# ScalarE's arithmetic and four kinds of VectorE instructions kept in the program's order in a selective-scan and attention kernel

## The chip, the cores and the metric

The kernel runs on one core of a Trainium2 chip. The metric is the device time of one execution in microseconds, as the median of several runs. A core has TensorE (PE, with its weight loads shown apart as PEld), VectorE (DVE), ScalarE (ACT), GpSimd (POOL) and SyncE (SP, which here only issues DMAs).

## The reference, cut to what matters

For 32 sequences of 256 tokens with 256 channels, the output is the input plus a two-layer feed of a conditioning block. The conditioning block is a gated state-space scan with 512 inner channels and 16 states; then come two layers of windowed attention (8 heads of 64, window 128) with a gated feed-forward of 682 hidden units. All in float32.

```python
# conditioning block, per sequence
xr, gate = split(x @ W_in.T);  xr = xr + t_emb
xc = silu(causal_conv4(xr) + b_conv)
xn = (xc - mean) / sqrt(var + 1e-5) * ln_g + ln_b
Bm, Cm, dt = split(xn @ W_xproj.T)
dt = tanh(dt @ W_dt.T + b_dt) * 0.01
Ad = 1 + dt * (-tanh(A_log));  Bd = Bm * minimum(norm(xn), 1)
for t in tokens:
    h = clip(h * Ad[t] + Bd[t] * xn[t], -10, 10);  y[t] = Cm[t] @ h
z = (y + D * xn) * silu(gate) @ W_out.T
# two layers, on z
q, k, v = split(shift(z) @ wqkv)
q, k = rotary(l2norm(q) * qs), rotary(l2norm(k) * ks)
z = z + windowed_softmax_attention(q, k, v) @ wo
a, g = split(layernorm(shift(z)) @ w1 + b1)
z = z + (a * gelu(g)) @ w2 + b2
out = x + z
```

## The kernel before, in words

**Two streams of work.** The 32 sequences are four groups of 8 (`GB`). The scan of a group runs over 256 tokens in 8 chunks of 32 (`group_scan`). Attention and feed-forward run over 64 positions, one for each group, layer and sequence (`seqs`). The first group is scanned alone; after that the scan of group g+1 is laid beside the positions of group g; the last group's positions have no scan beside them.

**How the order is written down.** In `group_scan` an agenda says at which scan step each piece is traced: `at(s0 - 36 + 2 * ch, conv_th, c, ch)` is the Tanh of chunk c, channel block ch, 36 steps before the chunk begins. For positions, `stage(n, i, what)` says in which of 8 slots of position n a piece is traced. The last loop of the program goes over the slots, traces what stands in each, and then lets the scan go on by about two steps, so that 16 positions go with 256 steps, or two with a chunk. So the text of the program gives one order over all engines.

**Who decides the order on an engine.** The order of the text is not the order of the queues. A scheduler reads the traced program, reckons by its own model when each operand will be there, and lets an instruction go ahead of earlier ones of its engine if it takes it to be ready. `tc.keep_in_program_order(ins)` puts an edge without a wait from the last instruction traced on the same engine to `ins`: `ins` may not be queued before that one. It says nothing of later instructions. In the kernel before it stands at some table set-up on GpSimd, and at `scale_row` (L645 to L652) for all groups but the first.

**The pieces that the change and the prediction name.**

- `conv_in` (L425 to L436) adds the condition to a projection in PSUM (DVE, xr) and starts the convolution (POOL, acc); `conv_taps` (L442) adds three taps on VectorE; `conv_th` (L450) is a Tanh on ScalarE, th; `conv_out` (L455) makes xc.
- `norm_turn` (L494) transposes xc into a PSUM bank tp_x; `norm_stats` (L504 to L509) takes mean and variance on VectorE and a power of -0.5 on GpSimd into stat; `norm_shift` (L514, DVE) multiplies mean and stat; `norm_apply` (L521, ACT) reads tp_x and writes xn; `norm_affine` (L528, L529, POOL) multiplies and adds; `norm_out` (L533, L535) stores xn in DRAM (xnd) by SP and squares it on ScalarE, sq_x. Each stands two to five steps after the one before it.
- `length` (L541, L542) ends in a power on GpSimd; `figures` (L550, DVE) makes rhs of it two steps later.
- `load_rows` (L625, SP) loads a token's row xrep from xnd, spread over states, six steps ahead; `scale_row` (L646, ACT) multiplies it by beta two steps ahead; `step` (L656, DVE) is the recurrence h; `read_out` (L668, PE) takes y from four h.
- `gate_th` (L368, L706, ACT) copies the gate out of PSUM (sg) and takes a Tanh (th_g); `copy_y` (L757, ACT) copies the block's output (yo); `raw_copy` (L472, ACT) copies raw.
- `Attention.project` (L903) is ps_qkv; v is copied on ScalarE (v_sb, L1084); `rotated` takes a square on ScalarE (sq, L916), the rotary products on VectorE (rot L919, swp L924), and three products and powers on GpSimd (L927, L935, L936); `turn` (L942, L947) transposes and copies into qT and kT on ScalarE.
- `scores` (L1102, L1109, L1118) ends in Exp on ScalarE (pT); `sums` (L1128, L1136) gives the inverse of the row sums; `values` (L1147, L1154) multiplies with v and copies into oT on ScalarE; `put_inverse` and `load_inverse` (L1159, L1166, SP) send the inverse through DRAM and back, spread over partitions, as rb, in slots 0 and 2 of the next position; `divide` (L1170, DVE) multiplies oT by rb in slot 4; `finish` (L953, L961) is ps_wo and the residual in slot 6.
- `FeedForward.normalise` (L1187 to L1197) ends in a power on GpSimd, rstd; `apply` (L1203, DVE) is hn; `spread` (L1215, L1217) transposes and writes hT on ScalarE; `widen` (L1238, L1246) is pa and a Gelu on ScalarE, ag; `product` (L1254, DVE) multiplies the two; `narrow` (L1266, L1277) is po_f and the residual on VectorE.

All PSUM tiles share one pool of eight banks (`ps_w`, tag "w"). xn, th and acc have two buffers each, xrep six, oT and rb one.

Of the kernel before, what the change touches and what calls it, by code (L numbers as in the profile page):

```python
# [13 lines left out]
AF = mybir.ActivationFunctionType  # L14
# [59 lines left out]
def kernel(  # L74
# [139 lines left out]
    for i in range(2):  # L214
        t = const.tile([P, NI * (P + GB)], FP, tag=f"ly{i}", name=f"ly{i}")
        nc.gpsimd.memset(t, 0.0)
        ly.append(t)

    def program(ctx, exact):
        rpool = ctx.enter_context(tc.tile_pool(name="res", bufs=1, reuse_waits="tile"))  # L220
        wpool = ctx.enter_context(tc.tile_pool(name="weights", bufs=1, reuse_waits="tile"))
# [12 lines left out]
        def constants(at):  # L234
# [75 lines left out]

            def decay_rate():

                nc.scalar.activation(a_sb, a_sb, AF.Tanh)
                nc.vector.tensor_scalar(a_sb, a_sb, -1.0, 0.01, ALU.mult, ALU.mult)

            def load_later():
# [48 lines left out]

        def reorder(out, ps):

            nc.scalar.copy(  # L368
                out.rearrange("p (q i b) -> p b i q", q=NQ, b=GB),
                ps.rearrange("p (b i q) -> p b i q", q=NQ, b=GB),  # L370
            )

        def group_scan(g):
# [73 lines left out]
            def conv_th(c, ch):  # L447
                acc = ck[c]["xr", ch][1]
                th = sp.tile([P, GB * CH], FP, tag="th", name="th", bufs=2)
                nc.scalar.activation(th, acc.rearrange("p b t -> p (b t)"), AF.Tanh, scale=0.5)  # L450
                ck[c]["th", ch] = th

            def conv_out(c, ch):
# [15 lines left out]

            def raw_copy(c):  # L470
                raw = sp.tile([4 * NS, GB * CH], FP, tag="raw", name="raw")
                nc.scalar.copy(raw, ck[c].pop("pr")[0 : 4 * NS, 0 : GB * CH])  # L472
                ck[c]["raw"] = raw

            def raw_turn(c):
# [35 lines left out]

            def norm_shift(c, j):
                stat, mv = ck[c]["stat"], ck[c].pop(("mv", j))
                nc.vector.scalar_tensor_tensor(  # L514
                    stat[:, j, 1:2], mv[:, 0:1], -1.0, stat[:, j, 0:1], ALU.mult, ALU.mult
                )

            def norm_apply(c, j):
                tp, stat = ck[c].pop(("tp", j)), ck[c]["stat"]
                xn = sp.tile([P, DI], FP, tag="xn", name="xn", bufs=2)  # L520
                nc.scalar.activation(  # L521
                    xn, tp, AF.Identity, bias=stat[:, j, 1:2], scale=stat[:, j, 0:1]
                )
                ck[c]["xn", j] = xn
# [6 lines left out]
            def norm_out(c, j):  # L531
                xn = ck[c].pop(("xn", j))
                nc.sync.dma_start(out=ck[c]["xnd"][j * P : (j + 1) * P], in_=xn)  # L533
                sq = sp.tile([P, DI], BF, tag="th", name="sq_x", bufs=2)
                nc.scalar.activation(  # L535
                    sq, xn, AF.Square, accum_out=ck[c]["ss"][:, j : j + 1]
                )

# [6 lines left out]
            def figures(c):  # L545
                stat = ck[c].pop("stat")
                ck[c]["rhs"] = []
                for j in range(NJ):
                    rhs = sm.tile([P, 3, CH], FP, tag="rhs", name="rhs")
                    nc.vector.tensor_mul(rhs, bc(tok_step, 1, 3), bc(stat[:, j], 2, CH))  # L550
                    ck[c]["rhs"].append(rhs)

            def figures_out(c):
# [26 lines left out]

            def decay_th(c):
                ad = sm.tile([P, CH], FP, tag="ad", name="ad")
                nc.scalar.activation(ad, ck[c]["bcd"][:, 2], AF.Tanh, bias=wbias[:, 2:3])
                ck[c]["ad"] = ad

            def decays(c):
# [113 lines left out]
            def gate_th(c, ch):  # L700
                if ch == 0:
                    ck[c]["sg"] = sp.tile([P, NC_, GB * CH], FP, tag="sg", name="sg")
                sg = ck[c]["sg"][:, ch]
                reorder(sg, ck[c].pop(("ps", NC_ + ch)))
                th = sp.tile([P, GB * CH], FP, tag="th", name="th_g", bufs=2)
                nc.scalar.activation(th, sg, AF.Tanh, scale=0.5)  # L706
                ck[c]["th_g", ch] = th

            def gate_out(c, ch):
# [44 lines left out]

            def copy_y(c, d):
                yo = sp.tile([P, GB, CH], FP, tag="yo", name="yo", bufs=2)
                nc.scalar.copy(  # L757
                    yo.rearrange("p b (i q) -> p q i b", q=NQ),
                    ck[c].pop(("po", d))[:, 0 : GB * CH].rearrange(
                        "p (q i b) -> p q i b", q=NQ, b=GB  # L760
                    ),
                )
                ck[c]["yo", d] = yo
# [148 lines left out]
        def rotated(l, ps, w, a):  # L912


            sq = ap_.tile([P, DI], FP, tag="swp", name="sq", bufs=3)
            nc.scalar.activation(sq, ps, AF.Square)  # L916
            rot = ap_.tile([P, HEADS, DH], FP, tag="rot", name="rot", bufs=4)
            ph = ps.rearrange("p (h d) -> p h d", h=HEADS)
            nc.vector.tensor_mul(rot, ph, bc(rc_sb[:, l, w, a], 1, HEADS))  # L919
            swp = ap_.tile([P, HEADS, DH], FP, tag="swp", name="swp", bufs=3)  # L920
            hd = DH // 2
            for i in range(2):
                o, s = slice(i * hd, (i + 1) * hd), slice((1 - i) * hd, (2 - i) * hd)
                nc.vector.tensor_mul(  # L924
                    swp[:, :, o], ph[:, :, s], bc(rs_sb[:, l, w, a, o], 1, HEADS)
                )
            nc.gpsimd.tensor_add(rot, rot, swp)  # L927
            ss = aw.tile([P, HEADS], FP, tag="ss", name="ss")
            nc.vector.tensor_reduce(
                ss, sq.rearrange("p (h d) -> p h d", h=HEADS), AX.X, ALU.add  # L930
            )

            nc.vector.tensor_scalar_max(ss, ss, 1e-24)  # L933
            rn = aw.tile([P, HEADS], FP, tag="rn", name="rn")
            nc.gpsimd.tensor_tensor(rn, ss, neg_half, ALU.pow)  # L935
            nc.gpsimd.tensor_mul(rot, rot, bc(rn, 2, DH))  # L936
            return rot

        def turn(rot, dst):
            tr = ps_w.tile([P, HEADS // 2, W], FP, tag="w", name="tr_qk")  # L940
            for hp_ in range(HEADS // 2):
                nc.tensor.transpose(  # L942
                    tr[:, hp_, :],
                    rot[:, 2 * hp_ : 2 * hp_ + 2, :].rearrange("p h d -> p (h d)"),
                    ident,
                )
            nc.scalar.copy(dst, tr)  # L947

        def project_out(b, oT):
            po = ps_w.tile([P, KM, S], FP, tag="w", name="ps_wo")  # L950
# [25 lines left out]
        def attention(l):  # L976

            for b in range(GB):

                qTs, kTs, vs = [], [], []  # L980
                for w in range(NW):
                    for a in (2, 0, 1):
                        ps = project_qkv(b, w, a)
                        if a == 2:
                            v_sb = ap_.tile([P, DI], FP, tag="v1", name="v_sb", bufs=3)
                            nc.scalar.copy(v_sb, ps)
                            vs.append(v_sb)
                            continue
                        rot = rotated(l, ps, w, a)
                        dst = ap_.tile(  # L990
                            [P, HEADS // 2, W], FP, tag="kT1" if a else "qT1",
                            name="kT" if a else "qT", bufs=3 if a else 2,
                        )
                        turn(rot, dst)
                        (kTs if a else qTs).append(dst)
                        yield

                oT = ap_.tile([P, NC_, S], FP, tag="oT", name="oT", bufs=1)
                for w in range(NW):
# [6 lines left out]
                    for h0 in range(0, HEADS // 2, nh):  # L1006
                        for r in range(2):
# [19 lines left out]
                                nmax[:, hsl], p_sb, AX.X, ALU.max, negate=True  # L1027
                            )
                            for i, h in enumerate(hs):
                                nc.scalar.activation(  # L1030
                                    p_sb[:, i, :], p_sb[:, i, :], AF.Exp,
                                    bias=nmax[:, h : h + 1],
                                    accum_out=rsum[:, h : h + 1],
# [34 lines left out]
        class Attention:  # L1068
# [7 lines left out]
            def project(self, b, w, a):  # L1076
# [4 lines left out]
                    ] + [ap_.tile([P, NW, DI], FP, tag="v", name="v_sb")]  # L1081
                ps = project_qkv(b, w, a)
                if a == 2:
                    nc.scalar.copy(self.qkv[b][2][:, w], ps)  # L1084
                else:
                    self.rot[b, w, a] = rotated(self.l, ps, w, a)

# [6 lines left out]
            def scores(self, b, kw, i0, n):  # L1094
# [20 lines left out]
                        )  # L1115
                for r in range(2):
                    p = aw.tile([P, n, nq], FP, tag="pT", name="pT", bufs=6)
                    nc.scalar.activation(p, banks[r], AF.Exp)  # L1118
                    for i in range(n):
                        self.p[b, kw, i0 + i, r] = p[:, i, :]  # L1120

# [17 lines left out]
            def values(self, b):  # L1139
                oT = ap_.tile([P, NC_, S], FP, tag="oT", name="oT", bufs=1)  # L1140
                for i0 in range(0, HEADS // 2, 2):
                    ov = ps_w.tile([P, 2, S], FP, tag="w", name="ov")
                    for i in range(2):
                        for kw in range(NW):
                            for r in range(2):
# [5 lines left out]
                                    start=(kw == 0),  # L1151
                                    stop=(kw == NW - 1),
                                )
                    nc.scalar.copy(oT[:, i0 : i0 + 2], ov)  # L1154
                self.o[b] = oT

            def put_inverse(self):
# [9 lines left out]
                self.rb = rb  # L1167

            def divide(self, b):
                nc.vector.tensor_mul(self.o[b], self.o[b], self.rb)  # L1170

            def finish(self, b):
                project_out(b, self.o.pop(b))
# [1 line left out]
        class FeedForward:  # L1175
# [24 lines left out]
            def apply(self, w):  # L1200
                tp, mv, rstd = self.hn[w]
                hn = ap_.tile([P, DM], FP, tag="hn", name="hn")
                nc.vector.tensor_scalar(  # L1203
                    hn, tp[:, 0:DM], mv[:, 0:1], rstd, ALU.subtract, ALU.mult
                )
                self.hn[w] = hn

            def spread(self, w):
# [5 lines left out]
                    ks = slice(k * P, (k + 1) * P)  # L1214
                    nc.tensor.transpose(tp[:, ks], hn[:, ks], ident)  # L1215
                for k in range(KM):
                    nc.scalar.activation(  # L1217
                        self.h[:, k, w * W : (w + 1) * W],
                        tp[:, k * P : (k + 1) * P],
                        AF.Identity,  # L1220
# [4 lines left out]
            def widen(self, m):  # L1225
# [17 lines left out]
                        stop=(k == KM - 1),  # L1243
                    )
                ag = aw.tile([P, S], FP, tag="ag", name="ag", bufs=7)
                nc.scalar.activation(ag[0:n], pg, AF.Gelu, bias=b1g)  # L1246
                self.pa[m] = pa, ag

            def product(self, m):
# [275 lines left out]
```

## Time and profile before

| | |
|---|---|
| median of 3 runs | 3857.5 us (3853.15 to 3862.57) |
| the profiled execution | 3861.79 us |
| span in its profile | 3860.0 us |
| PE busy | 3671.3 us, 95%, 20028 matmul records |
| PE weight loads | 2261.0 us, 59% |
| VectorE busy | 2629.5 us, 68%, 5177 instructions |
| ScalarE busy | 2163.9 us, 56%, 3769 instructions |
| GpSimd busy | 1754.4 us, 45%, 1776 instructions |
| DMA | 387.54 MB, 100 GB/s on average |
| the chain that ended last | PE 48%, DVE 20%, POOL 13%, DMA 8%, ACT 6%, issue 4% |

The profile is of one execution on the core. Its span runs from the first instruction to the last. A busy share is an average over stages with different limits. A line of a list of waits names the waiting engine and tile with its line of code, then an arrow to what came last, then the total in us, how often, and the longest. The chain of waits is followed back from the last instruction; in order of time its lines show a start, a length and what filled it. Ends of matmuls are modelled in such a profile, and matmuls overlap, so a busy PE is not a PE at its peak.

### The profile page before, as it was taken

How to read it: one execution, taken by the hardware profiler on the slowest of the kernel's cores; microseconds unless marked ns; L12 is line 12 of the kernel's file. 1: busy time of each engine (PE TensorE's matmuls, PEld its weight loads, DVE VectorE, ACT ScalarE, POOL GpSimd, SP SyncE). 2: the span in 40 equal slices, each digit the busy share in tenths (PEclk: the TensorE clock that was granted, in tenths of full speed). 3: DMA queues.
4: the chain of work that ended last, by engine and by line, in shares of the span. 5: the costliest groups of instructions: out<-in, count | busy, mean ns of one | idle time of the engine just before them, and what ended most of it. 6: DMA issues, size and time to landing. Idle time of an engine off the chain costs nothing.

```text
span 3860.0 us, 57026 instructions
## 1 busy us (share of the span) xinstructions
PE 3671.3 (95%) x20028; PEld 2261.0 (59%) x20028; DVE 2629.5 (68%) x5177; ACT 2163.9 (56%) x3769; POOL 1754.4 (45%) x1776
## 2 busy tenths in 40 slices
PE   7999889999999999999999999999999999999998
PEld 3333345665665665665666566566556666666666
DVE  6988887777777766777767677776777544444443
ACT  3555556565666656656655655565666444444442
POOL 4433465454454454454445445444444443443441
PEclk8999999999999999999999999999999999999999
DMA  5444554443444545334444544434344112011101
GB/s 152 115 118 117 145 140 120 111 117 98 117 125 118 139 115 140 106 99 113 107 120 110 128 121 128 120 95 111 105 117 126 51 45 62 12 28 37 30 25 35
DMA packets 396251, 387.54 MB, mean 100 GB/s; under 512 B 176355, under 2 KB 256052, under 8 KB 395828
## 3 DMA queue, kind: packets, MB, share of 16 engines
q1 hardware_dynamic: 311506, 371.80, 36.0%
q10 hardware_dynamic: 84450, 12.01, 2.0%
q8 instruction: 161, 2.64, 0.3%
q14 instruction: 134, 1.10, 0.1%
HBM read 348.05 MB, written 34.08 MB: 99 GB/s over the span
## 4 chain that ended last, share of the span: by engine, by line
PE 48%; DVE 20%; POOL 13%; DMA 8%; ACT 6%; issue 4%; SPq 1%; ACTq 0%; POOLq 0%; DVEq 0%
PE ps_qkv L903 9%; PE pa L1238 9%; PE po_f L1266 6%; DVE h L656 6%; POOL rn L935 5%; PE y L668 4%; DMA rb<-inv 3%; DVE acc L442 3%; PE ps_wo L953 3%; PE ov L1147 3%; PE sc L1109 3%; ACT xrep L646 2%; POOL rot L936 2%; DVE rot L919 2%; PE ps_in L395 2%
## 5 line engine op out<-in xcount | busy, mean ns | idle before, releaser
L656 DVE CUSTOM_DVE_ANT_0 h<-h,xrep,lim 128x512 f32<-128x512 f32 x1024 | 941.7, 920 | 133.8 <-ACT xrep L646 96.8
L903 PE MATMUL ps_qkv<-qkv,res 128*128 128x512 f32 x1536 | 715.0, 602 | 27.9 <-DVE ag L1254 18.2
L646 ACT ACTIVATE xrep<-xrep,beta 128x512 f32<-128x512 f32 x896 | 622.7, 718 | 139.3 <-DMA xrep<-xnd 99.1
L1238 PE MATMUL pa<-hT,w 128*128 128x256 f32 (+1 forms) x3072 | 684.5, 385 | 1.0 <-DVE zT L737 1.0
L1238 PEld LDWEIGHTS pa<-hT,w 128*128 128x128 f32 (+1 forms) x3072 | 497.8, 178 | 161.1 <-issue 42.3
L927 POOL TENSOR_TENSOR rot<-rot,swp 128x512 f32<-128x512 f32 x256 | 337.0, 1316 | 415.0 <-DVE swp L924 259.8
L935 POOL TENSOR_TENSOR rn<-ss,neg_half 128x8 f32<-128x8 f32 x256 | 453.4, 1771 | 28.0 <-DVE ss L933 17.5
L903 PEld LDWEIGHTS ps_qkv<-qkv,res 128*128 128x128 f32 x1536 | 278.9, 191 | 306.5 <-issue 263.0
L1266 PE MATMUL po_f<-ag,w 128*128 128x256 f32 (+1 forms) x1536 | 397.8, 401 | 40.0 <-DVE res L1277 16.6
L1197 POOL TENSOR_TENSOR rstd<-ve,neg_half 128x1 f32<-128x1 f32 x128 | 81.3, 635 | 771.3 <-DVE ve L1195 767.7
L668 PE MATMUL y<-h,ly 128*32 128x512 f32 x2048 | 381.1, 618 | 11.6 <-DVE h L656 10.9
L1254 DVE SCALAR_TENSOR_TENSOR ag<-pa,b_sb,ag 128x256 f32<-128x256 f32 (+1 forms) x448 | 213.0, 476 | 256.8 <-ACT ag L1246 254.3
L1266 PEld LDWEIGHTS po_f<-ag,w 128*128 128x128 f32 (+1 forms) x1536 | 279.7, 194 | 152.7 <-issue 43.6
L1246 ACT ACTIVATE ag<-pa,b_sb 128x256 f32<-128x256 f32 x320 | 150.7, 471 | 287.0 <-PE pa L1238 285.2
L936 POOL TENSOR_TENSOR rot<-rot,rn 128x512 f32<-128x512 f32 x256 | 294.5, 1150 | 20.0
L395 PE MATMUL ps_in<-xg,w_in_sb 128*128 128x256 f32 x1024 | 283.4, 406 | 15.1 <-DMA xg<-in_xT_dram 13.0
L916 ACT ACTIVATE sq<-ps_qkv 128x512 f32<-128x512 f32 x256 | 151.5, 596 | 238.9 <-PE ps_qkv L903 195.2
L395 PEld LDWEIGHTS ps_in<-xg,w_in_sb 128*128 128x128 f32 x1024 | 187.8, 197 | 146.8 <-issue 58.5
L442 DVE SCALAR_TENSOR_TENSOR acc<-xr,wc_sb,acc 128x256 f32<-128x256 f32 x384 | 187.8, 491 | 94.0 <-POOL acc L431 92.0
L953 PE MATMUL ps_wo<-oT,wo 128*128 128x256 f32 x1024 | 231.7, 379 | 0.0
L919 DVE TENSOR_TENSOR rot<-ps_qkv,rc_sb 128x512 f32<-128x512 f32 x256 | 175.0, 684 | 82.1 <-ACT sq L916 81.9
L1118 ACT ACTIVATE pT<-sc 128x512 f32<-128x512 f32 x384 | 208.5, 596 | 38.3 <-PE sc L1109 36.9
(146 smaller groups left out, 5479.9 us busy)
## 6 DMA issues: line engine op xcount, KB each, us to landing
xrep<-xnd SPq DMA_DIRECT2D x896, 256.0 KB
rb<-inv SPq DMA_DIRECT2D x128, 256.0 KB
xnd<-xn SPq DMA_DIRECT2D x64, 256.0 KB
qkv<-in_wqkv_dram SPq DMA_DIRECT2D x24, 512.0 KB
xd<-xnd SPq DMA_DIRECT2D x192, 64.0 KB
w<-in_w_dram SPq DMA_DIRECT2D x80, 128.0 KB
xg<-in_xT_dram SPq DMA_DIRECT2D x64, 128.0 KB
ys<-yo ACTq DMA_DIRECT2D x64, 128.0 KB
```

Of the source, the lines that this page charges most:

```text
L395: nc.tensor.matmul(ps, w_in_sb[:, k, ch * P : (ch + 1) * P], ck[c]["xg"][:, k], start=(k == 0), stop=(k == KM - 1),)
L442: nc.vector.scalar_tensor_tensor(acc, xr[:, :, k : k + CH], wc_sb[:, ch, k : k + 1], acc, ALU.mult, ALU.add,)
L646: scaled = nc.scalar.activation(bx, ck[c].pop(("bx", t), bx), AF.Copy, scale=ck[c]["beta"][:, t : t + 1])
L656: nc.vector._custom_dve(TENSOR_ADD_SAT, out=h_new, in0=state["h"], in1=bx, s0=ck[c]["lim"][:, 0, t : t + 1], s1=ck[c]["lim"][:, 1, t : t + 1],
L668: nc.tensor.matmul(ck[c]["y", hb][32 * q : 32 * q + 32, :], ly[hb % 2][:, 32 * t : 32 * t + 32], ck[c].pop(("h", hb * TB + t)), start=(i = ...
L903: nc.tensor.matmul(ps, res[b][:, k, t0 : t0 + W], wt["qkv", a][:, k], start=(k == 0), stop=(k == KM - 1),)
L927: nc.gpsimd.tensor_add(rot, rot, swp)
L935: nc.gpsimd.tensor_tensor(rn, ss, neg_half, ALU.pow)
L936: nc.gpsimd.tensor_mul(rot, rot, bc(rn, 2, DH))
L953: nc.tensor.matmul(po[:, d], wt["wo", 0][:, c, d * P : (d + 1) * P], oT[:, c, :], start=(c == 0), stop=(c == NC_ - 1),)
L1238: nc.tensor.matmul(pg if x else pa, wt["w1", m][:, k, x], self.h[:, k], start=(k == 0), stop=(k == KM - 1),)
L1266: nc.tensor.matmul(self.po[:, d], wt["w2", 0][r0 : r0 + n, m, d * P : (d + 1) * P], self.ag[m][r0 : r0 + n], start=(m == 0), stop=(m == le ...
```

## The change

Two small helpers, `activation` and `copy`, call ScalarE's instruction and pass it to `tc.keep_in_program_order`. All calls of `nc.scalar.activation` and `nc.scalar.copy` become calls of these, except in `scale_row`, which stays as it was: held for groups 1 to 3 and free for group 0. DMAs that ScalarE issues are not held themselves. Four kinds of VectorE instructions are held in the same way: `norm_shift` (L514), `figures` (L550), `divide` (L1170) and `apply` (L1203). Line numbers after the helpers grow by seven and more; on ScalarE the profile of the changed kernel shows the helpers' own lines.

```diff
+    def activation(*args, **kwargs):
+        return tc.keep_in_program_order(nc.scalar.activation(*args, **kwargs))
+
+    def copy(*args):
+        return tc.keep_in_program_order(nc.scalar.copy(*args))
...
             def conv_th(c, ch):
-                nc.scalar.activation(th, acc.rearrange("p b t -> p (b t)"), AF.Tanh, scale=0.5)
+                activation(th, acc.rearrange("p b t -> p (b t)"), AF.Tanh, scale=0.5)
...
             def norm_shift(c, j):
-                nc.vector.scalar_tensor_tensor(
-                    stat[:, j, 1:2], mv[:, 0:1], -1.0, stat[:, j, 0:1], ALU.mult, ALU.mult
+                tc.keep_in_program_order(
+                    nc.vector.scalar_tensor_tensor(
+                        stat[:, j, 1:2], mv[:, 0:1], -1.0, stat[:, j, 0:1], ALU.mult, ALU.mult
+                    )
                 )
...
             def norm_apply(c, j):
-                nc.scalar.activation(
+                activation(
                     xn, tp, AF.Identity, bias=stat[:, j, 1:2], scale=stat[:, j, 0:1]
                 )
...
             def figures(c):
-                    nc.vector.tensor_mul(rhs, bc(tok_step, 1, 3), bc(stat[:, j], 2, CH))
+                    tc.keep_in_program_order(
+                        nc.vector.tensor_mul(rhs, bc(tok_step, 1, 3), bc(stat[:, j], 2, CH))
+                    )
...
         def turn(rot, dst):
-            nc.scalar.copy(dst, tr)
+            copy(dst, tr)
...
             def divide(self, b):
-                nc.vector.tensor_mul(self.o[b], self.o[b], self.rb)
+                tc.keep_in_program_order(
+                    nc.vector.tensor_mul(self.o[b], self.o[b], self.rb)
+                )
...
             def apply(self, w):
-                nc.vector.tensor_scalar(
-                    hn, tp[:, 0:DM], mv[:, 0:1], rstd, ALU.subtract, ALU.mult
+                tc.keep_in_program_order(
+                    nc.vector.tensor_scalar(
+                        hn, tp[:, 0:DM], mv[:, 0:1], rstd, ALU.subtract, ALU.mult
+                    )
                 )
...
             def widen(self, m):
-                nc.scalar.activation(ag[0:n], pg, AF.Gelu, bias=b1g)
+                activation(ag[0:n], pg, AF.Gelu, bias=b1g)
```

The other replaced calls are those of `decay_rate`, `reorder`, `raw_copy`, `norm_out`, `decay_th`, `gate_th`, `copy_y`, `rotated`, `Attention.project`, `scores`, `values` and `spread`, and three in `attention`, which runs only where a bound on the scales of q and k does not hold; with these inputs it does not run.

## The prediction

> **What bounds the kernel now.** I read the busy times by stretch first, then the chain of waits in two places, then each engine's waits from 480 to 3000 us.
>
> ```profile
> 480.00:3000.00 2520.00, 2398.55 (x13599) 1519.86 (x13600) 1848.95 (x3611) 1512.68 (x2644) 1224.60 (x1211) 0.99 0.45 117
> 3000.00:3720.00 720.00, 719.82 (x4122) 480.72 (x4121) 326.11 (x701) 344.01 (x559) 303.04 (x258) 1.00 0.14 36
> 0.00:480.00 480.00, 423.62 (x1552) 166.54 (x1552) 405.31 (x762) 258.13 (x482) 196.51 (x280) 0.94 0.49 129
> ...
> 1584.68 0.70 PE po_f L1266 x2
> ...
> 1695.15 0.70 PE po_f L1266 x2
> ...
> 3304.78 3.45 PE ps_wo L953 x16
> ...
> 3346.35 3.45 PE ps_wo L953 x16
> ```
>
> The columns after the length are busy PE, PE weight loads, DVE, ACT and POOL. The run has three stages. To 480 us the scan of group 0 runs alone and VectorE is fullest (405 of 480). From 480 to 3000 us the scan of the next group runs beside attention and feed-forward: PE is busy 2398.55 of 2520 us, so it stands for 121.5 us, while VectorE is at 73% and ScalarE at 60%. From 3000 us on only attention and feed-forward are left, PE never stands, and a position (one sequence in one layer) takes 3346.35 - 3304.78 = 41.6 us. In the middle stage the chain repeats after two positions, 1695.15 - 1584.68 = 110.5 us, of which two bare positions are 83.1. The scan's matmul records per pair, at lengths from the same chain (64 of y at eight in 1.00, 16 of ps_out at eight in 1.94, 8 of ps_raw in 1.89, 32 of ps_in at four in 1.03, 16 of tz and tp_x at four in 0.59), fill about 24 us of the remaining 27. So a middle stage with no PE stall at all is worth about 3 us per pair where the pattern is regular, and 121.5 us with its irregular places. That is the ceiling of any gain there.
>
> ```profile
> PE ov L1147 <- DVE ag L1254: 21.9, 14, 2.6
> PE ps_qkv L903 <- DVE ag L1254: 18.2, 13, 1.4
> PE po_f L1266 <- DVE res L1277: 16.6, 10, 2.3
> ...
> DVE ag L1254 <- ACT ag L1246: 102.5, 60, 4.0
> DVE stat L514 <- POOL stat L509: 91.6, 39, 5.3
> DVE h L656 <- ACT xrep L646: 89.1, 81, 3.4
> DVE oT L1170 <- DMA rb<-inv: 82.8, 21, 5.8
> ...
> DVE rhs L550 <- POOL stat L542: 38.5, 23, 3.2
> DVE hn L1203 <- POOL rstd L1197: 34.1, 58, 1.8
> ...
> ACT th L450 <- DVE acc L442: 202.4, 68, 6.2
> ACT ag L1246 <- PE pa L1238: 141.9, 63, 6.8
> ACT sq L916 <- PE ps_qkv L903: 108.7, 100, 2.1
> ACT xn L521 <- DVE stat L514: 99.2, 36, 5.7
> ```
>
> These are total, times and longest wait in us, 480 to 3000. PE waits almost only for VectorE: its list adds up to 124 us, 104 of them on DVE, and mostly on a PSUM bank that VectorE has not yet read out. VectorE itself stands 649 us there: on four instructions whose input comes from GpSimd or a DMA (stat, oT, rhs, hn: 247), and on ScalarE (ag, h, and rot behind sq, 56.0: 248). ScalarE stands on th and xn, two scan instructions nobody is in a hurry for: I paired tiles in the trace, and between xn and the square that reads it lie 21 us in the median, between the division oT and the ps_wo matmuls more than 13 us in nineteen of twenty cases. These are heads of queues that hold up others and gain nothing.
>
> **What the Trainium skill says.** Perfetto Trace Analysis, "Tensor Engine Instruction (MATMUL, LD_WEIGHTS)": VectorE, ScalarE and GpSimd are strict FIFO, so a waiting head stops all behind it. The trace agrees: VectorE's 82.8 us before oT are idle though other work is queued. The same page, "Identifying the Most-Contended Engine": matmul busy time is no good measure of nearness to the limit. Here 95% PE busy hides the difference between the stages, which weight loads show (60% of the time in the middle, 67% after). PSUM — Partial Sum Buffer, "Terms": eight banks, a matmul output in one of them. From first matmul to last reader the trace has about 4.4 banks held on average in the middle stage, so a bank held longer is not at once a stall. ScalarE: Activation LUTs, "What ACT_TABLE_LOAD costs": about 1283 ns a load; the trace has 1283 ns, 248 times, 318 us.
>
> **The change, part by part.** No instruction is added or removed on any engine, and the built order has 248 table loads in both kernels: 0 us. Only orders move.
>
> ScalarE. All arithmetic but the 256 scale rows of group 0 (768 later ones were held already) now runs in the order of the text. Against before, in mean places of the queue: xn 10 later, th 3.2 later, sg and th_g 2 later, raw 2.2 later; sq 2.3, oT 3.0, qT and kT 2.6, ag 2.0 and v_sb 2.0 earlier. One instruction takes 1512.68/2644 = 0.57 us. Ten places are 5.7 us, against a mean wait of 99.2/36 = 2.8: the 99 us before xn go. th gets 1.8 us of cover against 202.4/68 = 3.0 us: about 60% of 202 goes, 122, and of the 43.1 us (13 times) that it waits behind ve about 20. That is 240 us of ScalarE's 1007 idle, 24%. They don't vanish, since ScalarE has work for 1513 us only: it will stand instead before PE's results (ag, sq, oT, qT), where it is early rather than late. VectorE's 248 us of waiting on ScalarE fall by the same 24%, 59 us.
>
> VectorE. In places: oT 18 later (2 to 36), stat 6.4 later, rhs 3.7 later, hn 1.3 earlier. One instruction takes 1848.95/3611 = 0.51 us. oT: 9.2 us of cover against a longest wait of 5.8, all 83 us go. stat: 3.3 us against 2.3 in the mean, about 80 of 91.6. rhs: 1.9 against 1.7, about 32 of 38.5. hn: nothing goes. Sum 195 us. What hides the lateness of oT is the reserve before ps_wo; were that gone, PE would wait for the division itself. With ScalarE's 59 that is 254 of 649 us, 39%.
>
> What PE gets. A share in proportion would be 39% of 121.5, 47 us; all of it 121.5. I take 60%, 73 us: the heads removed (2.3 to 3.9 us each) are longer than PE's waits (1.3 to 1.7 us each), so one removed head tends to remove a whole wait.
>
> GpSimd and SP. On SP the xnd write moves 4.3 places later, rb 0.8 earlier, the xrep loads 0.3 later; xn's two products on GpSimd move 3 later, rot 0.4 earlier. SP also waits in order, so an xnd write that comes late holds xrep loads; the 21 us after xn cover it. 0, at worst +10. Two banks per chunk (tp_x) are held some 15 us longer: 2 x 15 / 110 = 0.3 bank of eight; 0, at worst +15.
>
> First stage: VectorE bound, with 1.6 and 1.4 us of stat and rhs waits, so nothing to gain; th, waiting 45 us there, is not on VectorE's path. 0, from -10 to +15. Last stage: PE never stands, 0, at worst +10 if a strict ScalarE reaches an eviction late.
>
> Sum: -73. The profiled execution took 3861.8 us (span 3860.0), 4.3 above the median of the runs, so 3789 for it and 3857.5 - 73 = 3785 as a median.
>
> **Rivals.** *PE becomes the only bound* in the middle stage: -121.5, and some 30 more from matmuls following each other without restart: 3705. For it: after the change ScalarE waits for PE, not the reverse. Against: ag, h, hn and acc (76.9 behind GpSimd) still stop VectorE.
>
> *The waits are hidden anyway*: PE's stalls come from VectorE being 73% full in bursts, and with one head gone it stops at the next (acc, ag). Half the proportional share or less, -20: 3838. Against: 83 of the removed us are in single waits of 4 us.
>
> *Slower*: strict ScalarE puts the scale rows (L646) behind evictions that wait for PE. Per position four q/k turns and two oT copies have moved ahead; at 1.4 us of waiting each over 45 positions that is 378 us during which xrep is not made, and h (3.5 us of reserve in the median, under 0.8 in a quarter of its rows) stops VectorE. 378 - 195 = +183 us of VectorE waiting at 121.5/649 = 0.19 us each: +34, with +15 from the first stage and +10 from the last, 3917. It decides once VectorE's waits on ScalarE (248 us now) exceed 248 + 195 = 443.
>
> **How the numbers follow.** Forecast 0.52; PE bound 0.12; hidden 0.19; slower 0.17. The forecast's own range is 3740 to 3825. Leaving out the far halves of the two outer cases gives 3705 to 3880. About 0.2% (8 us) can be told from no change: of the hidden case a quarter lies within it, and a little of the slower one. Faster 0.77, same 0.07, slower 0.16.
>
> **What would show it.** oT, stat and rhs waits on VectorE near zero, th and xn waits on ScalarE cut by two thirds with ag, sq, oT and qT waits on PE grown; PE busy above 2440 per 2520 us in the middle; a pair of positions at 107 to 109 us; the last stage still 41.6 us a position. It is wrong if h behind xrep grows past 200 us, if PE waits on tp_x or ps_in banks, or if the last position starts no earlier.

## The result, and the profile after

| | before | after |
|---|---|---|
| median on the same chip | 3859.15 us (3853.15 to 3862.57, 4 runs) | 3802.81 us (3799.04 to 3807.15, 4 runs) |
| ratio | | 0.9856, 95% interval 0.9839 to 0.9873 |
| span of the profiled execution | 3860.0 us | 3805.3 us |
| PE busy, whole span | 3671.3 us | 3678.6 us |
| VectorE, GpSimd busy, whole span | 2629.5, 1754.4 us | 2685.8, 1845.0 us |

The change makes the kernel 56 us faster. First, the busy times by stretch after, from 480 us on (start and end, length, then busy PE, PE weight loads, DVE, ACT, POOL, the granted clock, the DMA share and GB/s):

```profile
480.00:3000.00 2520.00, 2467.15 (x13914) 1564.91 (x13913) 1938.76 (x3669) 1547.10 (x2692) 1329.27 (x1234) 0.99 0.46 117
3000.00:3720.00 720.00, 720.00 (x4163) 483.65 (x4163) 318.56 (x686) 339.83 (x553) 304.61 (x252) 1.00 0.14 36
```

PE now stands for 2520 - 2467.15 = 52.9 us in the middle instead of 121.5. Over the whole span (span less busy time) it stands for 126.7 us instead of 188.7, but is busy 7.3 us longer with the same 20028 matmul records. The last stage is full on PE, as before. The page's line for the chain that ended last, after:

```profile
PE 74%; DVE 14%; POOL 4%; ACT 3%; issue 2%; DMA 2%; SPq 0%; ACTq 0%; POOLq 0%; DVEq 0%
```

PE was 48% of it, GpSimd 13% and DMA 8%. The inverse sums on their way through DRAM (rb) are no longer in the chain; the powers on GpSimd (rn) still are, but seldom. The waits after, 480 to 3000 us (total, times, longest in us):

```profile
ACT ag L221 <- PE pa L1253: 272.7, 143, 5.1
ACT sq L221 <- PE ps_qkv L914: 147.8, 133, 1.8
DVE h L667 <- ACT xrep L657: 145.6, 109, 3.6
ACT oT L224 <- PE ov L1158: 134.0, 87, 7.2
...
DVE st L1204 <- PE tp_h L1200: 98.9, 40, 3.7
...
DVE rot L930 <- ACT sq L221: 63.4, 49, 2.9
...
ACT th L221 <- DVE acc L449: 37.5, 15, 6.6
...
DVE hn L1217 <- POOL rstd L1210: 31.6, 48, 3.1
DVE ag L1269 <- ACT ag L221: 29.2, 43, 2.5
...
DVE stat L522 <- POOL stat L516: 4.8, 2, 4.4
DVE rhs L560 <- POOL stat L551: 1.6, 1, 1.6
```

VectorE's wait for rb is gone from the list, and so is ScalarE's for the statistics before xn. ScalarE and VectorE now wait mostly for PE (ag, sq, oT; and st, which stood at 9.3 us before). One wait has grown that isn't on PE: h behind its scaled row xrep, from 89.1 to 145.6 us.

The chain in order of time after (start, length, what) repeats every 1662.66 - 1552.49 = 110.2 us in the middle, and every 41.6 us at the end:

```profile
1552.49 0.70 PE po_f L1281 x2
...
1662.66 0.70 PE po_f L1281 x2
...
3041.60 3.45 PE ps_wo L964 x16
3083.17 3.45 PE ps_wo L964 x16
```

In the regular places the pair was 110.5 us before, so it has hardly moved. What went are the irregular places. From the trace I took the start, in us, of the first ps_wo matmul of positions 14 and 40 (counted from 0), the same in each run below:

| | position 14 | position 40 | mean pair between |
|---|---|---|---|
| before | 1378.6 | 2848.7 | 113.1 us |
| after | 1351.7 | 2795.1 | 111.0 us |
| e1, all of ScalarE held, VectorE free | 1376.8 | 2833.3 | 112.0 us |
| e2, VectorE's four kinds held, ScalarE free | 1357.4 | 2773.3 | 108.9 us |
| e3, divide alone held | 1352.6 | 2794.0 | 110.9 us |
| e4, th and xn alone held | 1364.5 | 2783.1 | 109.1 us |
| e8, th, xn and divide held | 1339.8 | 2731.7 | 107.1 us |
| e5, th, xn and VectorE's four held | 1338.2 | 2724.8 | 106.7 us |
| e11, e5 with th free | 1339.9 | 2755.1 | 108.9 us |
| e7, e5 and the gate held | 1356.8 | 2746.3 | 106.9 us |
| e10, e5 and yo held | 1346.3 | 2731.7 | 106.6 us |
| e12, e5, gate and yo held | 1353.4 | 2793.3 | 110.8 us |
| e6, the change with gate and yo free | 1341.8 | 2727.6 | 106.6 us |
| e9, the change with yo free | 1344.5 | 2734.5 | 106.9 us |

"Mean pair" is the difference of the two columns over 13. Of what the change gains, 27 us are there by position 14 and another 27 come between 14 and 40. The twelve runs are told next.

### The profile page after: what moved, and what is told of

The parts are those of the page before. It is cut to its first block, busy times and chain, and to the rows that moved or that the text cites. A ratio compares the mean times of both kernels' runs of the same rounds, so it can differ in the third digit from the quotient of the medians.

```text
span 3805.3 us, 57114 instructions
## 1 busy us (share of the span) xinstructions
PE 3678.6 (97%) x20028; PEld 2274.6 (60%) x20028; DVE 2685.8 (71%) x5177; ACT 2170.2 (57%) x3769; POOL 1845.0 (48%) x1776
## 4 chain that ended last, share of the span: by engine, by line
PE 74%; DVE 14%; POOL 4%; ACT 3%; issue 2%; DMA 2%; SPq 0%; ACTq 0%; POOLq 0%; DVEq 0%
PE pa L1253 15%; PE ps_qkv L914 13%; PE po_f L1281 8%; PE y L679 6%; PE ps_wo L964 5%; DVE h L667 4%; PE ov L1158 4%; PE sc L1120 4%; PE ps_in L402 4%; PE ps_out L757 3%; PE tr_qk L953 3%; PE rs L1139 2%; DVE acc L449 2%; PE sc L1113 2%; DVE swp L935 1%
## 5 line engine op out<-in xcount | busy, mean ns | idle before, releaser
L667 DVE CUSTOM_DVE_ANT_0 h<-h,xrep,lim 128x512 f32<-128x512 f32 x1024 | 987.4, 964 | 182.9 <-ACT xrep L657 149.7
L1281 PE MATMUL po_f<-ag,w 128*128 128x256 f32 (+1 forms) x1536 | 389.9, 394 | 17.4 <-DVE ag L1269 14.9
L947 POOL TENSOR_TENSOR rot<-rot,rn 128x512 f32<-128x512 f32 x256 | 313.4, 1224 | 19.9
L449 DVE SCALAR_TENSOR_TENSOR acc<-xr,wc_sb,acc 128x256 f32<-128x256 f32 x384 | 188.7, 494 | 103.9 <-POOL acc L438 102.6
L1120 PE MATMUL sc<-qT,kT 64*128 64x128 f32 (+1 forms) x2048 | 239.2, 346 | 0.0
```

The costliest lines, as they stand in the source:

```text
L667: nc.vector._custom_dve(TENSOR_ADD_SAT, out=h_new, in0=state["h"], in1=bx, s0=ck[c]["lim"][:, 0, t : t + 1], s1=ck[c]["lim"][:, 1, t : t + 1],
L1120: nc.tensor.matmul(banks[r][:, i, :], kT[rows, i0 + i, kw * W : (kw + 1) * W], qT[rows, i0 + i, kw * W :], start=False, stop=(i == n - 1),)
L1281: nc.tensor.matmul(self.po[:, d], wt["w2", 0][r0 : r0 + n, m, d * P : (d + 1) * P], self.ag[m][r0 : r0 + n], start=(m == 0), stop=(m == le ...
```

## The experiments

**The two halves, and their likeliest parts.** Theory V: VectorE's heads (stat, rhs, oT, hn) carry the gain. Theory S: ScalarE's queue, freed of th and xn, carries it. e1 and e2 do one half of the change each.

```diff
 e1, against the change: each of the four VectorE kinds
-                tc.keep_in_program_order(
-                    nc.vector.tensor_mul(self.o[b], self.o[b], self.rb)
-                )
+                nc.vector.tensor_mul(self.o[b], self.o[b], self.rb)
 e2, against the change: ScalarE as it was
-        return tc.keep_in_program_order(nc.scalar.activation(*args, **kwargs))
+        return nc.scalar.activation(*args, **kwargs)
...
-        return tc.keep_in_program_order(nc.scalar.copy(*args))
+        return nc.scalar.copy(*args)
```

> All of ScalarE held, VectorE's four kinds free again. Theory V (the gain is VectorE's own four heads, 195 of the 254 us of waits in the prediction's sum, and a quarter of it ScalarE's): 10 to 20 us faster than before (ratio 0.995 to 0.997), VectorE's waits on oT, stat and rhs between 480 and 3000 us still near 83, 92 and 38 us. Theory S (the gain is ScalarE's queue freed of th and xn, so that Gelus, squares and copies come in time): 40 to 56 us faster (0.985 to 0.990), with the waits on oT, stat and rhs unchanged all the same.

> VectorE's four kinds held, ScalarE as before. Theory V: 35 to 50 us faster (0.987 to 0.991), waits on oT and stat near zero, and ScalarE still waiting some 200 us before th. Theory S: 5 to 15 us faster (0.996 to 0.999), since ScalarE still stands before th and xn and hands Gelus and squares to VectorE late. If the two parts need each other, both this and the run with ScalarE alone stay under half of the 56 us.

e3 is e2 with only `divide` held, e4 holds only th and xn and nothing on VectorE:

```diff
 e4, against e2 (VectorE's four free as well)
-                activation(th, acc.rearrange("p b t -> p (b t)"), AF.Tanh, scale=0.5)
+                tc.keep_in_program_order(
+                    activation(th, acc.rearrange("p b t -> p (b t)"), AF.Tanh, scale=0.5)
+                )
...
-                activation(
-                    xn, tp, AF.Identity, bias=stat[:, j, 1:2], scale=stat[:, j, 0:1]
+                tc.keep_in_program_order(
+                    activation(
+                        xn, tp, AF.Identity, bias=stat[:, j, 1:2], scale=stat[:, j, 0:1]
+                    )
                 )
```

> Only divide (oT by rb) held on VectorE, nothing else held. Theory V: its 83 us of waiting are 83/254 of the sum, so about 18 us faster (0.995), with the wait on rb near zero. Theory S: within 5 us of before, although the wait on rb goes: VectorE then stands at the next head (stat, ag, h) instead.

> Only the two ScalarE instructions th (conv_th) and xn (norm_apply) held, nothing on VectorE. Theory V: about 10 us faster (0.997). Theory S: 30 to 50 us faster (0.987 to 0.992), nearly all that holding the whole of ScalarE gives, because these two are the heads that stood in front of the others; waits of ScalarE before th and xn under a third of 202 and 99 us between 480 and 3000 us.

| | median | before, same chip | ratio, 95% interval |
|---|---|---|---|
| e1 | 3850.37 us | 3861.14 us | 0.9974 [0.9963, 0.9985] |
| e2 | 3774.20 us | 3861.14 us | 0.9776 [0.9763, 0.9789] |
| e3 | 3805.44 us | 3861.14 us | 0.9861 [0.9846, 0.9877] |
| e4 | 3798.76 us | 3861.14 us | 0.9846 [0.9828, 0.9864] |

VectorE's half alone gains 87 us, more than the whole change; ScalarE's half alone gains 11. So V had the order of these two right, and the size of e1; for e2 it had said 35 to 50. Neither theory had the other two: one VectorE kind alone (divide) gains 56 us, and two ScalarE kinds alone (th, xn) gain 62, where all ScalarE kinds gain 11. Nor did either foresee that in e1 VectorE's waits on oT, stat and rhs fall to 37.4, 68.0 and 19.1 us with nothing held there. Something among the other ScalarE kinds costs about 50 us. What VectorE's half leaves standing is seen in the waits of e2, 480 to 3000 us:

```profile
ACT th L221 <- DVE acc L449: 210.3, 72, 6.7
...
DVE h L667 <- ACT xrep L657: 203.2, 152, 3.4
...
ACT xn L221 <- DVE stat L522: 97.0, 26, 5.1
```

th and xn still stand at ScalarE's head as long as before (202.4 and 99.2), and h waits longer for its rows (203.2 us against 89.1). With th and xn alone held, e4, the same list has:

```profile
DVE stat L523 <- POOL stat L518: 88.5, 40, 5.3
...
DVE h L667 <- ACT xrep L657: 30.5, 34, 3.4
```

h waits a third as long as before, stat as long. The two repairs work on different waits.

**Only the parts that gained, and which part costs.** e5 holds th and xn (and one Tanh at set-up, `decay_rate`) on ScalarE and the four kinds on VectorE; all other ScalarE kinds are free. e6 is the whole change with sg, th_g and yo free, and so keeps attention's and the feed-forward's evictions held: theory E was that those evictions cost the 50 us. e7 is e5 with sg and th_g held. e8 is e5 with only `divide` held on VectorE.

```diff
 e6, against the change (e5 does the same to all kinds but th, xn and decay_rate)
-            copy(
+            nc.scalar.copy(
                 out.rearrange("p (q i b) -> p b i q", q=NQ, b=GB),
...
-                activation(th, sg, AF.Tanh, scale=0.5)
+                nc.scalar.activation(th, sg, AF.Tanh, scale=0.5)
...
-                copy(
+                nc.scalar.copy(
                     yo.rearrange("p b (i q) -> p q i b", q=NQ),
```

> The changed kernel with only th, xn (and the one-off decay rate) held on ScalarE; all other ScalarE instructions free, VectorE's four kinds held. Theory G (the part of the change that costs is holding the scan's other ScalarE work, above all sg, th_g and yo, which then stand in a burst right before a scale row): 90 to 105 us faster than before (0.973 to 0.977), a pair of positions at 107.5 us in the middle stage, VectorE's wait on xrep under 110 us between 480 and 3000 us. Theory C (th and xn held late are themselves the cost beside the four VectorE kinds, since xn late makes the chunk late): 45 to 65 us faster, as the whole change.

> The changed kernel with sg, th_g and yo free again on ScalarE; everything of attention and feed-forward still held. Theory G: 80 to 105 us faster than before (0.973 to 0.979). A rival, theory E (evictions of attention, moved ahead of scale rows, are the cost): no better than the change, 50 to 60 us faster, with VectorE's wait on xrep still above 140 us.

> th, xn and the gate's sg and th_g held on ScalarE, nothing else there; VectorE's four kinds held. Theory G with the gate as the piece: 50 to 70 us faster than before, so 30 to 45 us lost against the kernel with th and xn alone. Theory G with yo as the piece, or theory E: within 10 us of the kernel with th and xn alone.

> th and xn held on ScalarE, and of VectorE's kinds divide alone. If each head pays once, divide (56 us alone) and th with xn (62 us alone) would add up to 118 us; since PE stood for 121.5 us and the two share its waits I expect 75 to 95 us (0.975 to 0.981), and 5 to 20 us less than with all four kinds.

| | median | before, same chip | ratio, 95% interval |
|---|---|---|---|
| e5 | 3733.14 us | 3856.75 us | 0.9679 [0.9664, 0.9693] |
| e6 | 3738.78 us | 3856.75 us | 0.9693 [0.9679, 0.9707] |
| e7 | 3752.71 us | 3856.75 us | 0.9721 [0.9706, 0.9736] |
| e8 | 3739.44 us | 3856.75 us | 0.9692 [0.9678, 0.9705] |

e5 is the fastest version found: it beats the kernel before by 124 us and the change by some 68 (ratios 0.9679 and 0.9856). Theory G had said 90 to 105. e6 is within 6 us of it, inside the intervals, with every eviction of attention held, so theory E falls: with gate and yo free, the q/k turns, oT, sq and ag cost next to nothing in the text's order. The cost lies with the gate and yo. But the gate alone, e7, costs only 16 us by the ratios (0.0042; 20 by the medians), nearly all of it before position 14: the table has it 18.6 us behind e5 there and 21.5 at position 40. That is neither the 30 to 45 us of G with the gate as the piece nor the under 10 of its rivals.

e8 against e4 and e3: 62 and 56 us alone, 117 together, so th with xn and divide add up, where 75 to 95 had been expected. Stat, rhs and hn, worth 33 us on top of divide alone (e2 against e3: 0.0085), are worth 5 when th and xn are held (e5 against e8: 0.0013, inside the intervals).

**Where the cost sits in time.** I read one and the same place of the pair in the chain of the change and of e5, from the ps_qkv of four matmuls to the po_f matmuls. After (pieces left out between):

```profile
1595.08 1.93 PE ps_qkv L914 x4
...
1597.52 0.62 ACT yo L224
1598.13 0.49 ACT sg L224
...
1599.68 0.67 ACT xn L221
1600.35 0.62 ACT xrep L657
1600.99 1.73 DVE h L667
...
1608.49 0.49 DVE ag L1269
...
1612.18 0.70 PE po_f L1281 x2
```

and e5:

```profile
1570.93 1.72 PE ps_qkv L914 x4
...
1578.31 1.00 PE y L679 x8
1579.31 1.93 PE ps_in L402 x8
...
1582.98 2.98 PE po_f L1281 x12
```

From the end of ps_qkv to po_f the change needs 1612.18 - 1597.01 = 15.2 us, nearly all of them on ScalarE and VectorE; e5 needs 1582.98 - 1572.65 = 10.3, all on PE. ScalarE's own order there, after (start, length, engine and line, what, and in brackets the idle time before it with its releaser):

```profile
1589.09 0.72 ACT L657 ACTIVATE xrep<-xrep,beta 128x512 f32<-128x512 f32 x1
1593.05 0.47 ACT L221 ACTIVATE ag<-pa,b_sb 128x256 f32<-128x256 f32 x1 [3.24 <-PE pa L1253]
...
1597.04 0.58 ACT L224 COPY v_sb<-ps_qkv 128x512 f32<-128x512 f32 x1 [2.25 <-PE ps_qkv L914]
1597.52 0.62 ACT L224 COPY yo<-ps_out 128x256 f32<-128x256 f32 x1
...
1600.25 1.32 ACT L657 ACTIVATE xrep<-xrep,beta 128x512 f32<-128x512 f32 x2
```

and in e5:

```profile
1567.29 0.61 ACT L768 COPY yo<-ps_out 128x256 f32<-128x256 f32 x1 [2.32 <-PE ps_out L757]
...
1568.81 0.71 ACT L657 ACTIVATE xrep<-xrep,beta 128x512 f32<-128x512 f32 x1
...
1572.30 0.76 ACT L657 ACTIVATE xrep<-xrep,beta 128x512 f32<-128x512 f32 x1
1572.92 0.61 ACT L1095 COPY v_sb<-ps_qkv 128x512 f32<-128x512 f32 x1
```

The bank of yo is written by 1590.42 in the change (ps_out at 1588.50 for 1.92 us), but yo runs at 1597.52, because in the text it stands after the copy of v, and v waits for PE. The gate comes after yo, xn after the gate, and the next row xrep after all of them: 1589.09 to 1600.25 without a row. h stops, the products of VectorE behind it come late, and PE waits for the last of them. In e5 yo runs as soon as its bank is written, and rows go through between everything else. This recurs: between positions 14 and 40 yo starts 6.8 us after its bank is written in the median of 26 cases in the change, and 0.4 in e5.

**One link or the whole chain.** e9 frees yo alone in the change; e10 holds yo alone beside e5; e12 holds yo and the gate beside e5, with attention still free. e11 asks which of th and xn gains: it is e5 with th free.

```diff
 e9, against the change
-                copy(
+                nc.scalar.copy(
                     yo.rearrange("p b (i q) -> p q i b", q=NQ),
 e10, against e5
-                nc.scalar.copy(
+                copy(
                     yo.rearrange("p b (i q) -> p q i b", q=NQ),
 e12, against e10
-            nc.scalar.copy(
+            copy(
                 out.rearrange("p (q i b) -> p b i q", q=NQ, b=GB),
...
-                nc.scalar.activation(th, sg, AF.Tanh, scale=0.5)
+                activation(th, sg, AF.Tanh, scale=0.5)
 e11, against e5
-                activation(th, acc.rearrange("p b t -> p (b t)"), AF.Tanh, scale=0.5)
+                nc.scalar.activation(th, acc.rearrange("p b t -> p (b t)"), AF.Tanh, scale=0.5)
```

> The change with one kind of ScalarE instruction free again: copy_y (yo), everything else held. Theory Y (yo alone carries what e6 gave back: a held yo stands behind copies of later positions and keeps the scale rows waiting): ratio 0.970 to 0.975, about 3745 to 3760 us, pair of positions at 106.5 to 107, h waiting for xrep below 120. Rival G (gate and yo are only costly together, or gate alone puts the rows back): ratio 0.980 to 0.986, pair still near 110.

> e5 with copy_y (yo) held on ScalarE in addition. Theory Y: about 40 us lost against e5, ratio 0.977 to 0.981, pair at 109 to 110.5, most of it steady. Rival G: under 15 us lost, ratio 0.968 to 0.972, pair at 106.5.

> e5 without th held: only xn and decay_rate held on ScalarE, with the four VectorE kinds. e2 (neither held) and e5 (both) are 37 us apart. Theory P (each counts by the time it stood waiting in e2, th 210 and xn 97): ratio about 0.9745, 25 us above e5. Rival X (xn counts most, because its waits are the longest in one piece and the rows of the scan stand behind it): within 10 us of e5, ratio 0.968 to 0.9705.

> e5 with both copy_y (yo) and the gate (sg, th_g) held on ScalarE; attention, feed-forward, raw, ad and sq_x stay free. Alone, the gate cost about 16 to 20 us (e7) and yo about 12 (e10) over e5. Theory C (an unbroken chain: yo is held behind the copy of v, sg behind yo, th_g behind sg, so the rows after them are late too; with any link free the rest slips past): the steady pair goes back to 110, h waiting for xrep above 130, ratio 0.980 to 0.986, about 50 us over e5. Rival A (the two costs add): 30 us over e5, ratio 0.974 to 0.978, steady pair 106.5. Rival H (attention's held evictions are needed as well): within 15 us of e7, ratio 0.970 to 0.974.

| | median | before, same chip | ratio, 95% interval |
|---|---|---|---|
| e9 | 3742.14 us | 3851.50 us | 0.9720 [0.9700, 0.9739] |
| e10 | 3737.18 us | 3851.50 us | 0.9711 [0.9691, 0.9731] |
| e11 | 3766.09 us | 3851.50 us | 0.9787 [0.9767, 0.9807] |
| e12 | 3804.11 us | 3855.46 us | 0.9870 [0.9854, 0.9887] |

Freeing yo alone takes the change from 0.9856 to 0.9720, as theory Y said; yet holding yo alone costs e5 only 0.0032, about 12 us (the two intervals just overlap), as its rival G said. Both hold once the two are read together: it takes yo and the gate. e12 settles it. Gate 16 to 20 and yo 12 us would add up to some 30; together they cost 0.0191, 74 us, and the pair goes from 106.7 to 110.8. e12 stands at the time of the whole change though attention's kinds are free, and its chain has the same pieces at the same place:

```profile
1598.03 0.03 ACT v_sb L1095
...
1598.51 0.61 ACT yo L224
...
1601.33 0.62 ACT xrep L657
...
1601.98 1.74 DVE h L667
...
1613.18 0.70 PE po_f L1281 x2
```

Theory C stands, though the loss is above the 50 us it named; rivals A and H fall. The hold is an edge from the last instruction traced to the one held. With yo free, nothing ties the gate to v; with the gate free, nothing ties the rows to yo. Only where every link behind v is held does a wait for PE at v reach the row of the scan; v itself need not be held, and in e12 it is not. The order on ScalarE bears this out. Of the 26 yo between positions 14 and 40, 13, one in a pair, come directly after v in the change, in e12 and in e10. The gate's sg comes directly after yo in 13 cases in the change and in e12, but in none in e10, where yo is late too (6.2 us after its bank in the median).

What doesn't tell the cost is how long h waits for its rows in total: 151.1 us in e10 and 148.0 in e12, which is some 61 us slower (ratios 0.9711 and 0.9870), and 203.2 in e2, which is faster than e12 as well. It matters where h waits: in e12 and the change the chain of waits leaves PE at that place, in e5 and e10 it stays on PE.

What the single holds cost comes in the first positions and then stays; why it does was not looked into.

e11 missed both of its theories: with xn held and th free it is at e2's ratio (0.9787 against 0.9776). So with th free, holding xn adds nothing to VectorE's four kinds, although ScalarE's wait before xn goes from 97.0 us in e2 to 2.7: that wait covered nothing that matters there. The 37 to 42 us between these and e5 come with th, which in e11's trace still stands 206.3 us at ScalarE's head. Whether th alone would do without xn was not run.

## Why the prediction came out right, and where its steps did not

**The direction and the size.** Predicted -73, measured -56, inside the forecast's own range. PE's rise (2467 busy of 2520 us), the last stage (41.6 us a position) and the first stage (position 1 begins at 632.5 us instead of 632.1) came as said. The right total was made of parts that were off in opposite directions, so that it fits so well is in part luck.

**VectorE's heads: right in waits, too small in time.** stat, oT, rhs and hn stood 247 us and stand 4.8 + 0 + 1.6 + 31.6 = 38, so 209 went where 195 were named, hn staying as said. In the sum these were 195/254 of 73, 56 us; alone they gave 87 (e2). The division alone was 83/254 of 73 = 24 us in the sum and gave 56 (e3). The term that was mis-sized is what PE gets for a wait: in e2 the four stand 30.6 + 0 + 0 + 40.2 = 71 us, so 176 us of waiting gone were worth 87 us, 0.49 us for each, where the sum had 73/254 = 0.29; for the division it was 56 of 83, 0.67. Taken on the whole change the step's 60% came out: in the middle PE stands 121.5 - 52.9 = 68.6 us less, but its busy time grew. Two readings behind the step were a little off: rhs, at 38.5/23 = 1.7 us a wait, is no longer than PE's own waits, and the reserve between division and ps_wo is over 13 us in 58 of 64 cases, not nineteen of twenty.

**ScalarE's heads: right in place, and lumped with what costs.** "xn gone" came true (99.2 to none), th fell by more than the 60% said (202.4 to 37.5), and ag, sq and oT wait longer for PE, as said. But the step went on to take 24% off all of VectorE's waits on ScalarE, 59 us, which in the sum is 17 us of time. Measured, those waits fell by 9: ag 102.5 to 29.2, rot 56.0 to 63.4, h 89.1 to 145.6. th and xn by themselves gave 62 us (e4), and the gate and yo took 74 back (e12 against e5). On top of VectorE's half, the ScalarE half costs 31 us (0.9776 to 0.9856). An average over a queue said nothing of which instruction ends up in front of which.

**The slower rival** had the mechanism: a strict ScalarE puts scale rows behind evictions that wait for PE, and h stops VectorE. It had the wrong place and size. It named the q/k turns and oT copies, which cost about nothing with gate and yo free (e6). The place is v, yo and the gate, once in a pair, and the price of 74 us stays under what th, xn and the four kinds bring (124 in e5). Its mark, VectorE's waits on ScalarE over 443 us, was not reached: 238.

**The ceiling** of 121.5 us and the pair of 107 to 109. The pair in the change is 110.2, outside; e5 gains 124 us with PE still standing 2520 - 2491.55 = 28.5 us in the middle, so the ceiling was none. The step took PE's busy time for a fixed amount of work. Over one pair, by stretch, the change and then e5 show:

```profile
1552.49:1662.66 110.17, 108.92 (x616) 69.74 (x616) 84.82 (x163) 67.06 (x118) 57.21 (x54) 1.00 0.39 101
```

```profile
1529.31:1635.76 106.45, 106.26 (x617) 68.68 (x617) 83.17 (x163) 66.97 (x118) 56.47 (x54) 1.00 0.40 105
```

The same matmuls (within one record) at the same clock are "busy" for 108.92 us in one and 106.26 in the other, where the whole pair is over in 106.45. PE's matmuls at this place, one pair later, in the change and then in e5:

```profile
1704.21 1.05 PE L679 MATMUL y<-h,ly 128*32 128x512 f32 x2
...
1712.77 1.06 PE L679 MATMUL y<-h,ly 128*32 128x512 f32 x6
...
1716.54 1.16 PE L1120 MATMUL sc<-qT,kT 64*128 64x128 f32 x8
...
1718.40 1.16 PE L1120 MATMUL sc<-qT,kT 64*128 64x128 f32 x8
```

```profile
1684.69 1.06 PE L679 MATMUL y<-h,ly 128*32 128x512 f32 x8
...
1688.26 1.16 PE L1120 MATMUL sc<-qT,kT 64*128 64x128 f32 x16
```

Two y matmuls take as long as six or eight, and eight sc matmuls as long as sixteen. The records show why: a y matmul fills 32 of the array's 128 columns (128*32 in the list), and in a full group four start within 0.03 us of each other; an sc matmul fills 64 of its 128 rows, and two start within 0.01 us. Where one part's input or bank is late, or the scheduler puts other work between, the parts run one after the other, and each is busy for the full time. In the pair at 1552 us this makes up 1.0 us (y) and 1.2 us (sc) of the 2.66.

Over the whole run the same 20028 matmuls are busy for 3671.3 us before, 3678.6 in the change, 3674.3 in e12 and 3630.4 in e5. Counted in the records, the change has 49 whole sc groups of sixteen and e5 64; y runs in 348 stretches in the change and in 331 in e5. At the two prices above that is, as an estimate, 35 of the 48 us by which the change is busy longer than e5; the rest is open. So of the 74 us that the change's profiled execution is longer than e5's, about two thirds stand in PE's busy time and one third in its idle time (126.7 against 100.8). "No PE stall" was therefore no floor for the time. The rival "PE becomes the only bound" had put 30 us for matmuls in closer sequence; between the kernel before and e5 PE's busy time fell by 40.9.

## What to carry to other kernels

Hold in order the few instructions that stand at a queue's head with others waiting behind them (here th and the division, 117 us together with xn), not a whole engine: in this kernel an order chain carried a late producer's wait to the row at its end, and did so only where no link behind that producer was free. Before adding such edges, follow from each held instruction back to the last one that waits for another engine, and see whether a loop-carried input, here the row of a recurrence, stands behind it. Test halves and parts in combination: two holds that cost 12 and 16 to 20 us alone cost 74 together. And don't take busy time of PE for a fixed amount of work where small matmuls run side by side.

## What was not expected of the hardware

The recurrence h takes longer while GpSimd is at work. The groups by line, before and after (busy in us and mean in ns, then idle before it):

```profile
L656 DVE CUSTOM_DVE_ANT_0 h<-h,xrep,lim 128x512 f32<-128x512 f32 x1024 | 941.7, 920 | 133.8 <-ACT xrep L646 96.8 <-DVE h L656 6.4 <-PE y L668 2.5
```

```profile
L667 DVE CUSTOM_DVE_ANT_0 h<-h,xrep,lim 128x512 f32<-128x512 f32 x1024 | 987.4, 964 | 182.9 <-ACT xrep L657 149.7 <-DVE h L667 9.2 <-PE ps_out L757 0.9
```

The same 1024 instructions cost 46 us more in the change. I sorted them by whether a GpSimd instruction is on record during them: without one, h takes 804 ns in the mean before and 806 after; with GpSimd busy all along, 1057 and 1175 ns, with up to 1.9 us for one. Before, 475 of the 1024 ran with GpSimd idle, after only 335. GpSimd's own busy time rose from 1754.4 to 1845.0 us with the same 1776 instructions. This agrees with the Trainium skill, SBUF — State Buffer, "SBUF: two separate sides": a VectorE instruction with two inputs in SBUF and a GpSimd one that reads there take a shared pair of ports by turns, each for a whole instruction. GpSimd's spans are rough in such a profile, and no run took its work away, so how much of the 46 us is this lock is a reading, not shown. The prediction counted every VectorE duration as fixed.
